# Layer 0's weight products as seven block products, and a plan with other lags, slots and tie-breaks, in a four-layer graph network

## The chip, the core and the metric

The kernel runs on one core of one Trainium2 chip. The metric is the device time of one execution in microseconds (us). The engines named below are PE (TensorE, which streams a moving operand past weights that PEld loads), DVE (VectorE), ACT (ScalarE), POOL (GpSimd) and SP, whose queue issues nearly all DMAs. The matmul outputs lie in eight PSUM banks of 128 x 512 float32.

## The reference

Input `x` is 64 graphs of 256 nodes with 128 features, float32; `adj` is one 256 x 256 matrix for all. Four layers follow one another, each with a residual and a layer norm:

```python
x = layernorm(x + L0(x, adj, adj, weight_1))   # sum over k of (adj^k x) W_k, k = 0..3, two chains
x = layernorm(x + L1(x, adj, weight, bias))    # adj (x W) + b
x = layernorm(x + L2(x, adj, W, b))            # normalised (adj + I) x W^T + b
x = layernorm(x + L3(x, adj, adj, ...))        # five gated steps, weights shared
# one step of L3
m_in = adj @ h; m_out = adj @ h; av = [m_in, m_out]
z = sigmoid(av @ w3.T + b3 + h @ u3.T + bu)
r = sigmoid(av @ w4.T + b4 + h @ u3.T + bu)
hv = tanh(av @ w5.T + b5 + (r * h) @ u5.T + bu5)
h = (1 - z) * h + z * hv
```

Both chains of L0 have the same `adj`, so the kernel adds their weights: four matrices w_0 to w_3 of 128 x 128 remain (w_0 with the identity, for the residual), and the sum is x w_0 + adj x w_1 + adj^2 x w_2 + adj^3 x w_3.

## The kernel before

Everything is float32. The 64 graphs are 32 groups of two (`NB`). A group's tile is 128 partitions x 512: two graphs, two node tiles of 128, 128 features. `Group.record` writes down a group's whole way through the four layers as operations on an engine with a cost, a lag until the result can be used, and the values they read and write. `Plan.order` then places all operations of all groups in one list: it goes from one free moment to the next and takes, over the engines, the operation that can start first, then the one of lowest rank (older groups first). Values of a kind share a fixed number of slots (`slots`: 8 banks, 48 SBUF tiles of 128 x 512 named "w", and others); a value holds its slot from its first user to its last. Each engine runs its own operations in the order of that list. Up to 10 groups (`ACTIVE`) are in flight, so PE has other groups' work while one group waits.

Layer 0, for a group. `propagate("q", x, a2T)` makes qT = (adj^2 x)^T in tile `mq`. Groups 0 and 2 (`near`, the first `HEAD` graphs) have x turned on PE (`ptx`); for the 30 others DVE turns 32 x 32 blocks (`tx`, L745), a DMA writes them to DRAM (`dx`, L748) and two DMAs bring them back as `xT` (L753), with the features in a permuted order, for which four DMAs (L308) make a permuted copy `w0p` of w_0 and w_1 at the start. Then, for each of two node tiles, a bank `py` takes x [w_0 w_1] + q [w_2 w_3], 256 columns wide: per graph one matmul with x as the stationary operand and one with q. ACT copies the right half into `v` (L771), PE adds adj v to the left half (`py<-v,aT`), and ACT copies the result to `s0` (L783). The sum is centred beforehand in the weights (`centre(w0s, w0m)` on DVE), so the layer norm needs ACT squares with an accumulator (L515), POOL's add of EPS and power -0.5 (L519, L520) and an ACT scaling (L531).

`propagate` itself is, for groups of two, `seven`: a 2 x 2 block product in seven 128 x 128 products instead of eight, with sums of x made on POOL (L614 to L621), sums of the matrix made once on DVE (`s_aT`, `s_a2T`, `s_anT`, `s_aTp`, L355 to L359), and sums of the results on DVE and ACT (L642 to L664). Its first product is an operation of its own, before the three that need POOL's sums. Layers 1 and 2 are one `seven` and one product with the weights each.

A step of layer 3: `seven` gives `mg`; bank `pr` takes w4 mg + u3 hT; ACT writes r into an SBUF tile (`gate_`, L722); DVE makes rh = r hT (L729); bank `ph` takes w5 mg and u5 rh; `pr` takes (w3 - w4) mg on top, and so holds z's argument; z and tanh are written in place into the banks; DVE forms the new hT; a DVE transpose and DMAs through DRAM bring it back with nodes on partitions (`packed`). The last `END` graphs end in `closing`, on PE, ACT, POOL and DVE.

The start: `a_nat` and x loads, then the weights, all on SP in the order of the plan; `aTp` (four DMAs at L317) is a row-permuted copy of adj's transpose for the later steps; `ahat`, `dinv`, `p_an` and `anT` are the normalised matrix for layer 2.

Of the kernel before, what the change touches and what calls it, by code (L numbers as in the profile page):

```python
# [8 lines left out]
F32 = mybir.dt.float32  # L9
# [4 lines left out]
P = 128  # L14
NB = 2
ACTIVE = 10
# [34 lines left out]
class Plan:  # L51
# [32 lines left out]
    def order(self):  # L84
# [14 lines left out]
        while any(ready.values()):  # L99
            best = None  # L100
            for e, waiting in ready.items():
                t0 = free.get(e, 0.0)
                pick = None
                for at, op in waiting:
                    need = {}
                    for v in placed[op]:
                        if v.slot is None:
                            need[v.kind] = need.get(v.kind, 0) + 1
                    short = False
# [7 lines left out]
                    key = (max(at, t0), op.rank, op.seq)  # L117
# [5 lines left out]
            (start, _, _), op = best  # L123
# [34 lines left out]
def kernel(  # L158
# [42 lines left out]
    SHAPES = {"bank": [P, 512], "x": [P, 512], "w": [P, 512], "th": [P, 384], "q": [P, P], "st": [P, Q * 6], "mv": [P, Q * 2],  # L201
              "ve": [P, Q], "rs": [P, Q]}
    slots = {"bank": BANKS, "x": ACTIVE + 3, "w": 48, "th": 10, "q": 10, "dram1": 8, "dram2": 16, "st": 12, "mv": 12, "ve": 24, "rs": 12}
# [18 lines left out]
    def fetch(rank, o, src, v, queue, after=()):  # L222
        e, cost = QUEUES[queue]
        return pre(rank, queue, cost, lambda: e.dma_start(o, src), [], [v], lag=3000, joint=True, after=after)

    def load(rank, name, shape, src, keep=True, queue="SP"):
        v = constant(name, shape) if keep else Val("w", shape, name)
        e, cost = QUEUES[queue]
        pre(rank, queue, cost, lambda: e.dma_start(v.ap, src), [], [v], lag=3000 if queue != "SP" else 2300)
        return v  # L230
# [4 lines left out]
    nc.vector.memset(half, -0.5)  # L235

# [45 lines left out]
    w0_raw = load(-1, "w0_raw", [P, C, K0], w0)  # L282
# [21 lines left out]
    w0p = constant("w0p", [P, 2, C])  # L304

    def permuted():
        for r in range(4):
            nc.sync.dma_start(w0p.ap.rearrange("(j r) k c -> r j k c", r=4)[r], w0s.ap[32 * r:32 * (r + 1), 0:2, :])  # L308

    pre(1.2, "SP", 1800, permuted, [w0s], [w0p])  # L310
# [32 lines left out]
    pre(0.3, "DVE", 600, rows, [ahat, dinv], [ahat])  # L343
    pre(0.3, "PE", 4 * 110, lambda: turn(p_an, ahat), [ahat], [p_an])
# [34 lines left out]
    raw = {name: load(0.6, f"raw_{name}", [P, src.shape[1]], src, False, "SP")  # L379
# [60 lines left out]
    class Group:  # L440
# [68 lines left out]
        def spread_of(self, tag, s):  # L509
# [3 lines left out]
            def squares():  # L513
                for q in range(self.q):
                    nc.scalar.activation(nat(y)[:, q, :], nat(s)[:, q, :], AF.Square, scale=C ** -0.5,  # L515
                                         accum_out=ve.ap[:, q:q + 1])

            def scales():
                nc.gpsimd.tensor_scalar(ve.ap, ve.ap, EPS, None, op0=OP.add)  # L519
                nc.gpsimd.tensor_tensor(rs.ap, ve.ap, half[:, :self.q], op=OP.pow)  # L520

            self.act(squares, [s], [y, ve], 295 * self.q)
            self.add("POOL", 1330, 100, scales, [ve], [ve, rs])
# [22 lines left out]
        def normalise(self, tag, s, mv, rs):  # L546
# [8 lines left out]
            return y  # L555

# [36 lines left out]
        def seven(self, tag, h, aTs, ins, blocks):  # L593
# [32 lines left out]
            def first():  # L626
                block(0, ins(h)[:, 0, 0], aTs.ap[:, 0, :P], True)

            def middle():
# [24 lines left out]
            started = self.pe(pe_cost(P, 1), first, [h, aTs], [ps])  # L654
            kept = self.act(lambda: nc.scalar.copy(row(u, 1), row(ps, 0)), [ps], [u], 165)
# [3 lines left out]
            self.pe(pe_cost(P, 3), middle, [ts, sums], [ps], True, (started,))  # L659
# [39 lines left out]
        def packed(self, name, src):  # L699
# [13 lines left out]
            self.add("SP", 900, 2300, run, [far], [t])  # L713
# [5 lines left out]
        def gate_(self, name, ps, func, bias, kept=True):  # L719

            t = self.val("w", name) if kept else ps
# [10 lines left out]
        def record(self):  # L732
            x_ = self.val("x", "x")
            plan.add("SP", 450, 4500 if self.start < HEAD else 2700, self.rank() - 1.5, lambda: nc.sync.dma_start(nat(x_), self.view(x)), [], [x_],
# [3 lines left out]
            if near:  # L738
                xT, w01 = self.copied("xT", self.transposes("x", x_)), w0s
            else:  # L740

                w01 = w0p
                turn, far = self.val("w", "tx"), self.val("dram", "dx")
                xT = self.val("w", "xT")
                self.dve(lambda: nc.vector.transpose(  # L745
                    turn.ap.rearrange("p (r b i t) -> p r b t i", r=4, t=T, i=32),
                    x_.ap.rearrange("p (b t r j) -> p r b t j", r=4, t=T, j=32)), [x_], [turn])
# [9 lines left out]
            v, s0 = self.val("w", "v"), self.val("w", "s0")  # L757
            py = []

            for t in range(T):  # L760
                p = self.val("bank", f"py0{t}")
                py.append(p)

                def first(p=p, t=t):
                    for b in range(self.nb):
                        o = p.ap[:, b * 2 * C:(b + 1) * 2 * C]
                        mm(o, (tiles if near else pairs)(xT)[:, b, t], w01.ap[:, 0:2, :], b == 0, True, shared=True)
                        mm(o, tiles(qT)[:, b, t], w0s.ap[:, 2:4, :], False, True, shared=True)

                def moved(p=p, t=t):  # L770
                    nc.scalar.copy(parts(v)[:, t], four(p)[:, :, 1, :])  # L771

                self.pe(pe_cost(2 * C, 2 * self.nb), first, [xT, qT, w01, w0s], [p])
                self.act(moved, [p], [v], 55 + 107 * self.nb)
            for t in range(T):

                def second(p=py[t], t=t):
                    for kt in range(T):
                        mm(four(p)[:, :, 0, :], aT.ap[:, kt, t * P:(t + 1) * P], parts(v)[:, kt],
                           False, True, shared=True)  # L780

                def summed(p=py[t], t=t):
# [130 lines left out]
```

## Time and profile before

| | |
|---|---|
| median of 3 runs | 1353.37 us (1351.7 to 1353.72) |
| profiled execution | 1352.22 us, of which the span from first to last instruction is 1350.3 us |
| granted PE clock | 0.999 of full |
| DVE busy | 940.9 us, 2304 instructions |
| ACT busy | 758.1 us, 2421 instructions |
| POOL busy | 680.7 us, 1097 instructions |
| DMA | 134.96 MB, 34% of 16 engines' time |
| PE busy in 0 to 10, 20 to 40, 40 to 1340, 1340 to 1350.3 us | 7.5, 17.4, 1298.2, 3.4 us |

A line of a group of instructions has the source line, the engine, output and inputs, the shape and the count; after the bar the summed busy time, the mean time of one in ns, and the engine's idle time just before them with what ended most of it. A float32 matmul stands in the trace as two passes, so an x640 in the page is 320 products; the ends of passes are modelled and overlap the next pass, so the cost of a product on PE is read from start to start. Everything before 40 us is the filling of the pipeline; after that PE's busy share is 99% to 100% in every stretch until 1340 us.

### The profile page before, as it was taken

What the parts mean: (1) busy time and instruction counts of PE and PEld (TensorE: products, weight loads), DVE (VectorE), ACT (ScalarE), POOL (GpSimd) and SP (SyncE); (2) the same over time, 40 slices, a digit from 0 to 9 for tenths busy, and PEclk for the clock granted to TensorE, in tenths of its full rate; (3) what the DMA queues carried; (4) which work ended last, traced back from release to release, by engine and by line L of the source; (5) the groups of instructions that cost most, each with busy time, mean ns of one, the idle gap of its engine ahead of it and who ended that gap; (6) DMA issues with size and microseconds to landing.
All of it is one profiled execution on the core that took longest, in us unless ns stands there. A gap on an engine that the chain in (4) does not pass through costs nothing.

```text
span 1350.3 us, 22012 instructions
## 1 busy us (share of the span) xinstructions
PE 1336.5 (99%) x6553; PEld 928.3 (69%) x6553; DVE 940.9 (70%) x2304; ACT 758.1 (56%) x2421; POOL 680.7 (50%) x1097
## 2 busy tenths in 40 slices
PE   8999999999999999999999999999999999999997
PEld 7886666676776766677666666676776776565554
DVE  5466677767667667865676776676666677877776
ACT  4675536467654556556565554474655686444445
POOL 5785425266742566247266443383653686233323
PEclk9999999999999999999999999999999999999999
DMA  6322334242522333333233433341332223333323
GB/s 175 109 71 71 94 94 128 77 128 78 147 78 77 111 95 118 115 106 100 64 110 110 127 100 98 94 137 56 110 102 63 82 85 121 87 106 95 93 78 110
DMA packets 269495, 134.96 MB, mean 100 GB/s; under 512 B 175776, under 2 KB 241056, under 8 KB 269376
## 3 DMA queue, kind: packets, MB, share of 16 engines
q1 hardware_dynamic: 269120, 133.42, 34.1%
q8 instruction: 53, 0.87, 0.3%
q14 instruction: 66, 0.54, 0.1%
q0 software_dynamic: 256, 0.13, 0.1%
HBM read 67.31 MB, written 65.80 MB: 99 GB/s over the span
## 4 chain that ended last, share of the span: by engine, by line
PE 95%; DVE 1%; DMA 1%; ACT 1%; issue 0%; SPq 0%; POOLq 0%; ACTq 0%; POOL 0%; DVEq 0%
PE pr L199 31%; PE ph L199 20%; PE pmg L199 19%; PE py L199 15%; PE pm L199 7%; PE pmq L199 3%; DMA x<-in_x_dram 1%; DMA w_raw<-in_L_gnn_weight_dram 0%; PE s L199 0%; DMA dx<-tx 0%; ACT y L515 0%; ACT y L551 0%; DVE s L543 0%; SPq L748 0%; DVE tx L745 0%
## 5 line engine op out<-in xcount | busy, mean ns | idle before, releaser
L199 PE MATMUL pr<-mg,w435u5T 128*128 128x512 f32 x640 | 319.8, 593 | 0.0
L614 POOL TENSOR_TENSOR tsg<-h 128x256 f32<-128x256 f32 x128 | 97.2, 760 | 292.5 <-DMA h<-dh 197.5
L722 ACT ACTIVATE r<-pr,bsum 128x512 f32<-128x512 f32 x160 | 109.7, 685 | 151.5 <-PE pr L199 150.7
L722 ACT ACTIVATE pr<-pr,bsum 128x512 f32<-128x512 f32 x160 | 105.5, 660 | 112.4 <-PE pr L199 109.3
L729 DVE TENSOR_TENSOR rh<-r,hT 128x512 f32<-128x512 f32 x160 | 122.7, 767 | 61.6 <-ACT r L722 60.7
L199 PE MATMUL ph<-rh,w435u5T 128*128 128x512 f32 x320 | 163.6, 594 | 0.0
L199 PE MATMUL ph<-mg,w435u5T 128*128 128x512 f32 x320 | 163.3, 592 | 0.0
L199 PE MATMUL pr<-hT,w2u3T 128*128 128x512 f32 x320 | 163.0, 593 | 0.0
L729 DVE TENSOR_TENSOR d<-ph,hT 128x512 f32<-128x512 f32 x160 | 109.7, 686 | 76.1 <-ACT ph L722 73.0
L199 PEld LDWEIGHTS pr<-mg,w435u5T 128*128 128x128 f32 x640 | 109.4, 191 | 65.3 <-issue 53.3
L722 ACT ACTIVATE ph<-ph,bsum 128x512 f32<-128x512 f32 x160 | 105.6, 660 | 60.4 <-PE ph L199 59.9
L531 ACT ACTIVATE y<-s,rs 128x128 f32<-128x128 f32 x384 | 122.1, 392 | 11.0 <-POOL rs L520 10.7
L515 ACT ACTIVATE y<-s 128x128 f32<-128x128 f32 x396 | 116.7, 299 | 16.9 <-DVE s L538 14.9
L199 PEld LDWEIGHTS pmg<-s_aTp,tsg 128*128 128x128 f32 x768 | 101.8, 192 | 33.5 <-issue 28.5
L652 DVE TENSOR_TENSOR mg<-pmg,usg 128x256 f32<-128x256 f32 x160 | 67.0, 419 | 72.7 <-PE pmg L199 70.4
L199 PEld LDWEIGHTS pmg<-aTp,h 128*128 128x128 f32 x512 | 87.1, 197 | 39.4 <-issue 29.2
L729 DVE TENSOR_TENSOR pr<-pr,d 128x512 f32<-128x512 f32 x157 | 108.7, 692 | 1.5
L520 POOL TENSOR_TENSOR rs<-ve,half 128x4 f32<-128x4 f32 x99 | 104.1, 1052 | 8.3
L519 POOL TENSOR_SCALAR ve<-ve 128x4 f32<-128x4 f32 x99 | 23.2, 234 | 166.6 <-ACT y L515 166.3
L729 DVE TENSOR_TENSOR hT<-hT,pr 128x512 f32<-128x512 f32 x157 | 106.1, 676 | 1.3
L199 PE MATMUL pmg<-s_aTp,tsg 128*128 128x128 f32 x768 | 106.2, 275 | 0.0
L642 DVE TENSOR_TENSOR usg<-usg,pmg 128x128 f32<-128x128 f32 x160 | 45.2, 284 | 81.7 <-PE pmg L199 47.7
(181 smaller groups left out, 2816.9 us busy)
## 6 DMA issues: line engine op xcount, KB each, us to landing
dh<-th SPq DMA_DIRECT2D x160, 256.0 KB, 2.0
h<-dh SPq DMA_DIRECT2D x256, 128.0 KB, 2.5
x<-in_x_dram SPq DMA_DIRECT2D x32, 256.0 KB, 3.4
hT<-dh SPq DMA_DIRECT2D x128, 64.0 KB, 2.0
out_dram<-y SPq DMA_DIRECT2D x32, 256.0 KB, 2.3
dx<-tx SPq DMA_DIRECT2D x30, 256.0 KB, 2.6
xT<-dx SPq DMA_DIRECT2D x60, 128.0 KB, 2.6
dn<-tn SPq DMA_DIRECT2D x29, 256.0 KB, 2.1
```

The costliest lines, as they stand in the source:

```text
L199: nc.tensor.matmul(o, lhsT, rhs, start=start, stop=stop, skip_group_check=shared)
L515: nc.scalar.activation(nat(y)[:, q, :], nat(s)[:, q, :], AF.Square, scale=C ** -0.5, accum_out=ve.ap[:, q:q + 1])
L519: nc.gpsimd.tensor_scalar(ve.ap, ve.ap, EPS, None, op0=OP.add)
L520: nc.gpsimd.tensor_tensor(rs.ap, ve.ap, half[:, :self.q], op=OP.pow)
L531: nc.scalar.mul(nat(y)[:, q, :], nat(s)[:, q, :], rs.ap[:, q:q + 1])
L614: nc.gpsimd.tensor_tensor(ts.ap[:, :2 * P].rearrange("p (x c) -> p x c", x=2), ins(h)[:, 1], ins(h)[:, :, 0], op=OP.subtract)
L642: nc.vector.tensor_tensor(row(u, 0), row(u, 1), row(ps, 3), op=OP.add)
L652: nc.vector.tensor_tensor(o(m, slice(1, 3)), o(ps, slice(1, 3), False), both, op=OP.add)
L722: self.act(lambda: nc.scalar.activation(t.ap, ps.ap, func, bias=bias[1], scale=1.0), [ps, bias[0]], [t], act_cost(self.width) + 100)
L729: self.dve(lambda: nc.vector.tensor_tensor(out(t), way(a), way(b), op=op), [a, b], [t])
```

## The change

- Layer 0's weight products for the 30 later groups go into a new `inner_seven`: a seven-product scheme over the 2 x 2 block of weights. DVE makes four sums of x and q (`sd`, `ss`, `se`, `sf`, in a new kind of slot "h" of 128 x 256), PE runs seven products of 128 columns per graph, and DVE and ACT put the results together in five additions and two copies. Sums of the weights (`w0t`) are made once on DVE. Groups 0 and 2 keep the old code, now in a function `inner`.
- DVE's transpose of x (now L852 of the changed kernel) reads with another order of the features, so that `xT` comes back in natural order; `w0p` and its four DMAs are gone.
- EPS goes into the squares as a bias `root` (the rows are centred, so the cross term sums to zero); POOL's addition is gone.
- In `seven` the first product joins the three behind POOL's sums.
- r of a step goes into a bank of its own instead of an SBUF tile.
- The plan: among operations of one engine that can start at the same time, one that opens no new bank comes ahead of one that does, and only then does rank count. 12 groups in flight; 38 "w" slots, 21 "h", 12 "th" and "q" in place of 48, none, 10 and 10. Costs and lags of loads, transposes and squares are other numbers. `rows` and `p_an` get later ranks.

```diff
-ACTIVE = 10
+ACTIVE = 12
...
+                        elif v.kind == "bank":
+                            opens = 0
...
-                    key = (max(at, t0), op.rank, op.seq)
+                    key = (max(at, t0), opens, op.rank, op.seq)
...
-    slots = {"bank": BANKS, "x": ACTIVE + 3, "w": 48, "th": 10, "q": 10, "dram1": 8, "dram2": 16, "st": 12, "mv": 12, "ve": 24, "rs": 12}
+    slots = {"bank": BANKS, "x": ACTIVE + 3, "w": 38, "th": 12, "q": 12, "h": 21, "dram1": 8, "dram2": 16, "st": 12, "mv": 12, "ve": 24, "rs": 12}
...
-    w0_raw = load(-1, "w0_raw", [P, C, K0], w0)
+    w0_raw = load(-1, "w0_raw", [P, C, K0], w0, lag=7300)
...
-    pre(1.2, "SP", 1800, permuted, [w0s], [w0p])
+    def w0_blocks():
+        w_0, w_1, w_2, w_3 = (w0s.ap[:, k, :] for k in range(4))
+        t1, t2, t3, t4 = (w0t.ap[:, k, :] for k in range(4))
+        nc.vector.tensor_sub(t1, w_1, w_0)
+        nc.vector.tensor_sub(t2, w_3, t1)
+        nc.vector.tensor_sub(t3, w_3, w_1)
+        nc.vector.tensor_sub(t4, w_2, t2)
+
+    pre(1.2, "DVE", 1000, w0_blocks, [w0s], [w0t])
...
-    pre(0.3, "DVE", 600, rows, [ahat, dinv], [ahat])
-    pre(0.3, "PE", 4 * 110, lambda: turn(p_an, ahat), [ahat], [p_an])
+    pre(0.9, "DVE", 600, rows, [ahat, dinv, w0s], [ahat])
+    pre(1.1, "PE", 4 * 110, lambda: turn(p_an, ahat), [ahat], [p_an])
...
                     nc.scalar.activation(nat(y)[:, q, :], nat(s)[:, q, :], AF.Square, scale=C ** -0.5,
-                                         accum_out=ve.ap[:, q:q + 1])
+                                         bias=root[:, 0:1], accum_out=ve.ap[:, q:q + 1])
...
-                nc.gpsimd.tensor_scalar(ve.ap, ve.ap, EPS, None, op0=OP.add)
...
+            self.add("DVE", 450, 400, s3, [xT], [sd])
+            self.add("DVE", 450, 400, s1, [xT, qT], [ss])
+            self.add("DVE", 450, 400, s2, [xT, ss], [st_])
+            self.add("DVE", 450, 400, s4, [qT, st_], [sf])
+
+            def opening():
+                times(half(out_, 0), at(xT, 0), w0s.ap[:, 0, :], True)
+                times(half(more, 0), whole(st_), w0t.ap[:, 1, :], True)
+                times(half(more, 1), whole(ss), w0t.ap[:, 0, :])
...
+            self.pe(pe_cost(P, 3 * NB), opening, [xT, ss, st_, w0s, w0t], [out_, more])
+            self.act(lambda: nc.scalar.copy(u1.ap, out_.ap[:, :N]), [out_], [u1], 270)
+            self.pe(pe_cost(P, NB), lambda: times(half(out_, 0), at(qT, 0), w0s.ap[:, 2, :]), [qT, w0s], [out_])
+            self.pe(pe_cost(P, NB), lambda: times(half(out_, 1), at(qT, 1), w0t.ap[:, 3, :]), [qT, w0t], [out_])
+            add(lambda: (u2.ap, u1.ap, more.ap[:, :N]), [u1, more], [u2])
+            self.pe(pe_cost(P, NB), lambda: times(half(more, 0), whole(sd), w0t.ap[:, 2, :]), [sd, w0t], [more])
+            add(lambda: (u3.ap, u1.ap, more.ap[:, :N]), [u1, more], [u3])
+            add(lambda: (half(v, 1), whole(u3), half(more, 1)), [u3, more], [v])
+            self.pe(pe_cost(P, NB), lambda: times(half(more, 1), whole(sf), w0s.ap[:, 3, :]), [sf, w0s], [more])
+            add(lambda: (half(v, 0), whole(u2), half(more, 1)), [u2, more], [v], True)
+            for t in range(T):
+
+                def second(t=t):
+                    for kt in range(T):
+                        mm(half(out_, t), aT.ap[:, kt, t * P:(t + 1) * P], half(v, kt), False, True, shared=True)
+
+                self.pe(pe_cost(N, T), second, [v, aT], [out_])
+            self.act(lambda: nc.scalar.copy(s0_t(0), half(out_, 0)), [out_], [s0], 270)
+            add(lambda: (s0_t(1), whole(u3), half(out_, 1)), [u3, out_], [s0], True)
...
-            def first():
+            def opening():
                 block(0, ins(h)[:, 0, 0], aTs.ap[:, 0, :P], True)
-
-            def middle():
                 block(2, row(ts, 0), sums.ap[:, 0, :])
...
-            t = self.val("w", name) if kept else ps
+            t = self.val("w" if kept is True else "bank", name) if kept else ps
...
-            plan.add("SP", 450, 4500 if self.start < HEAD else 2700, self.rank() - 1.5, lambda: nc.sync.dma_start(nat(x_), self.view(x)), [], [x_],
+            plan.add("SP", 450, (6000, 9000)[self.start // NB] if self.start < HEAD else 2700, self.rank() - 1.5, lambda: nc.sync.dma_start(nat(x_), self.view(x)), [], [x_],
...
-                    x_.ap.rearrange("p (b t r j) -> p r b t j", r=4, t=T, j=32)), [x_], [turn])
+                    x_.ap.rearrange("p (b t j r) -> p r b t j", r=4, t=T, j=32)), [x_], [turn], 1000)
...
+            s0 = (self.inner if near else self.inner_seven)(xT, qT)
...
-                r = self.gate_(f"r{s}", pr, AF.Sigmoid, rb)
+                r = self.gate_(f"r{s}", pr, AF.Sigmoid, rb, "bank")
```

In the changed program's order of instructions DVE makes `s_aT`, `s_a2T`, then the sums `w0s`, then `s_aTp`, and only then centres `w0s`; before, the sums and the centring of `w0s` came ahead of all four. PE takes `p_an` after the first weight products of groups 0 and 2; before, it stood ahead of them. SP's order up to the four `aTp` DMAs and the next two loads of x is unchanged.

## The prediction

> **What bounds the kernel now.** I read the page's busy times, then its chain of waits, then the list of PE's waits, then a stretch of PE's timeline from start to start, and last the first 25 us. The first two say which engine sets the time:
>
> ```profile
> PE 1336.5 (99%) x6553; PEld 928.3 (69%) x6553; DVE 940.9 (70%) x2304; ACT 758.1 (56%) x2421; POOL 680.7 (50%) x1097
> ...
> PE 95%; DVE 1%; DMA 1%; ACT 1%; issue 0%; SPq 0%; POOLq 0%; ACTq 0%; POOL 0%; DVEq 0%
> ```
>
> PE is busy 99% and carries 95% of the chain that ends last; no other engine is over 70%. A busy PE may still be slowed, so the waits of PE count (waiter, what it waited for, us in total, times, longest):
>
> ```profile
> ...
> PE pmq L199 <- ACT mq L664: 1.3, 1, 1.3
> PE p_an L259 <- DVE ahat L334: 1.2, 1, 1.2
> PE pm L199 <- DVE m L648: 1.0, 2, 0.7
> PE py L199 <- DVE m L652: 0.6, 1, 0.6
> ...
> ```
>
> The nine entries of that list add up to 6.8 us, most of it in the first 41 us. So what is taken from PE's work comes off the time, and what is added to other engines costs only what makes PE wait. The price of PE's work is the distance from one start to the next (start, duration, what runs, passes):
>
> ```profile
> 701.10 0.39 PE L199 MATMUL pmg<-s_aTp,tqg 128*128 128x128 f32 x2
> 701.33 0.39 PE L199 MATMUL pm<-aT,y 128*128 128x128 f32 x2
> 701.55 0.60 PE L199 MATMUL py<-w0p,xT 128*128 128x256 f32 x2
> 701.99 0.59 PE L199 MATMUL py<-w0s,mq 128*128 128x256 f32 x2
> 702.42 0.59 PE L199 MATMUL py<-w0p,xT 128*128 128x256 f32 x2
> ```
>
> A product of 128 columns takes 0.22 to 0.23 us of PE, one of 256 takes 0.43. Over the whole timeline the medians are 0.223, 0.432 and (512 columns) 0.859 us; products whose stationary operand is read with a step of two elements (`pmg<-aTp,h`) take 0.235.
>
> **The weight products (30 groups).** Removed: 8 products of 256 columns a group, 8 x 0.432 = 3.456 us. Added: 14 of 128 columns. Two have x itself as stationary operand, with that step of two: 2 x 0.235; the other twelve read DVE's packed sums or q: 12 x 0.223. Together 3.146 us. The second products (`py<-v,aT`, 256 columns) stay. Saved: 0.310 us a group, 9.3 us in all. Ends: if all fourteen cost 0.235, 0.166 a group, 5.0 us; if all cost 0.223, 0.334, 10.0 us. I take 9.3, since each kind has its own row.
>
> The Trainium skill speaks against this term: its page "TensorE: Matmul & The Clock Gate", section "Back-to-back issue gap", says that in a real stream of weight load and matmul pairs a product of 128 columns is spaced at about 81 ns where its columns alone need 56, because the weight load binds too. An estimate with that ratio of 1.45 on 128 columns would make fourteen products 14 x 0.216 x 1.45 = 4.4 us, more than the eight they replace, and this term +28 us instead of a saving. The rows above don't show it for these float32 pairs: 0.223 is 3% over half of 0.432.
>
> **What the new scheme puts on DVE and ACT.** DVE, a group: four sums from SBUF to SBUF, 128 x 256. The trace has 419 ns for this size with one input in a bank (`mg`, L652), and for 512 columns 767 (both in SBUF) against 686 (one in a bank), so I take 419 x 767/686 = 468 ns (ends 419 and 767); and five additions with an input in a bank, 419 each. That is 4.0 us, 119 us for 30 groups. ACT loses four copies of 370 ns and gets two. Transposes of x with the new order: the row has 699 ns, and the new reading order isn't in the trace; between no change and twice the row I take 1.0 us, +9 us (ends 0 and +21). All this lies beside PE with 12 groups in flight: DVE goes from 941 to about 1055 us, 79% of the span. Without that cover every one of the four DVE steps between q and `v` would be paid, 2 x 0.47 + 2 x 0.42 = 1.8 us a group.
>
> **Squares, EPS and r.**
>
> ```profile
> L722 ACT ACTIVATE r<-pr,bsum 128x512 f32<-128x512 f32 x160 | 109.7, 685 | 151.5 <-PE pr L199 150.7
> L722 ACT ACTIVATE pr<-pr,bsum 128x512 f32<-128x512 f32 x160 | 105.5, 660 | 112.4 <-PE pr L199 109.3
> L729 DVE TENSOR_TENSOR rh<-r,hT 128x512 f32<-128x512 f32 x160 | 122.7, 767 | 61.6 <-ACT r L722 60.7
> L729 DVE TENSOR_TENSOR d<-ph,hT 128x512 f32<-128x512 f32 x160 | 109.7, 686 | 76.1 <-ACT ph L722 73.0
> ...
> L531 ACT ACTIVATE y<-s,rs 128x128 f32<-128x128 f32 x384 | 122.1, 392 | 11.0 <-POOL rs L520 10.7
> L515 ACT ACTIVATE y<-s 128x128 f32<-128x128 f32 x396 | 116.7, 299 | 16.9 <-DVE s L538 14.9
> ```
>
> A square with a bias read from SBUF should cost what the scaling with a scale read from SBUF costs, 392 in place of 299 ns: 396 x 0.093 = 37 us of ACT. POOL loses 99 additions of 234 ns, 23 us. r into a bank: 685 to 660 ns on ACT, and rh 767 to 686 on DVE, as the in-place row and d's row show; 4 and 13 us. ACT ends near 768 us, 57%, hidden under PE but for the last group, where nothing covers it: the four squares (0.25 us apart) become four of 0.35, +0.4 us, and the addition that started 0.31 us ahead of the power goes. Tail: +0.1 us, ends 0 and +0.4.
>
> r's bank is a resource that the old trace does not show used so. One bank is held from ACT's r to the end of DVE's rh: at the end of the run 1328.19 to 1329.60, 1.4 us; 160 x 1.4 = 226 bank-us of 8 x 1350, 2%. Following every bank tile in the timeline from first matmul to last reader gives about 6.5 of 8 banks in use on average, much of it by tiles that merely lie (a `pmq` is held 42 us), and the merged first product of `seven` and the new tie-break open banks later. Ends: -1 us (all PE waits after 60 us, 0.36 + 0.3 + 0.3, gone) and +8 us (each of 160 steps loses 50 ns, a quarter of one product). I take 0, nearer to the rows, as no PE wait of the list names a bank's release.
>
> The skill's page "ScalarE: Activation LUTs", section "Step-by-step: what each stage is for", says that ACT writes faster to a bank than to SBUF, but that this is useful only if TensorE doesn't need most of the banks, which is the case here. The rows confirm the first half (25 ns); with the second half alone the sum would lean to the +8 end.
>
> **The start.** Here the change moves a due step behind another, and I expect a loss.
>
> ```profile
> 8.43 0.39 DVE L287 TENSOR_TENSOR w0s<-w_raw,ident 128x128 f32<-128x128 f32 x1 [3.27 <-DMA w_raw<-in_L_gnn_weight_dram]
> ...
> 11.07 0.69 DVE L298 TENSOR_TENSOR w0s<-w0s,w0m 128x512 f32<-128x512 f32 x1
> ...
> 18.47 0.28 DVE L355 TENSOR_TENSOR s_aTp<-aTp 128x128 f32<-128x128 f32 x1
> ```
>
> ```profile
> 9.22 2.45 SPq L317 DMA_DIRECT2D aTp<-aT  x4
> ```
>
> Now the centred `w0s` is there at 11.8 and PE starts the weight products at 14.57. In the new order the centring stands behind `s_aTp`, and that waits for the four `aTp` DMAs, whose place on SP is the same: the last is issued at 11.1 and lands 2.1 to 3.0 us later, 13.2 to 14.1. Then five DVE operations of 1.07 us in all and the centring's three of 1.53 us: `w0s` at 15.8 to 16.7, say 16.2. Until then PE has p_a (8.2), x's transposes (2 x 0.43) and two `pmq` (2 x 1.73): done at 13.0. PE then waits 3.2 us, starts the products at 16.3 instead of 14.57, and still owes `p_an` (0.65): +2.4 us, ends +1.9 and +2.9. Behind the waiting DVE queue stand `both_w`, `rows`, `wb`, `w0t` and the first transposes of x, so `dx`, the next x loads (behind `dx` on SP) and `xT` start about when they did (20.9), not earlier, although SP is rid of 2.4 us of `w0p` DMAs.
>
> Between 29 and 41 us PE now waits 1.3 + 0.7 + 0.6 + 0.3 = 2.9 us on such chains. In the new order the first seven products need `se`, which DVE makes behind two transposes that wait for x loads (3.1 to 6.9 us to landing); by the same rows `se` is ready at about 34, when PE asks for it. I put 2.0 us in place of the 2.9: -0.9, ends -2.9 (none) and +2.5.
>
> **The sum** on the profiled execution: -9.3 - 0 + 0.1 + 2.4 - 0.9 = -7.7 us, 1352.2 to 1344.5 us (span 1342.6). The median of the runs is 1.15 us above that execution, so 1353.4 - 7.7 = 1345.7 us is forecast. All low ends together: -10.0 - 1 + 0 + 1.9 - 2.9 = -12.0, 1341.4; all high ends: -5.0 + 8 + 0.4 + 2.9 + 2.5 = +8.8, 1362.2.
>
> **Rivals.**
> 1. *Everything saved, and a clean start* (1341.4 us, the low ends). For it: 12 groups give PE more to choose from, and the lags in the plan come nearer to the 3.1 to 6.9 us of the trace. Against it: the wait for `aTp` is in the program's order.
> 2. *DVE's queue becomes the wait of the first 60 us* (1352.8 us). DVE runs strictly in order; in the old start it stood 3.18 and 1.37 us before a transpose until x came. If four such stops (2 x 4.55 = 9.1 us) come through to PE in place of the 2.9: -9.3 + 2.4 - 2.9 + 9.1 + 0.1 = -0.6. For it: DVE is 98% busy from 10 to 20 us and gets nine operations more a group; against it: PE has `pm` and `pmq` of other groups then.
> 3. *Banks run out: slower.* At the opening product of a step PE waits for a bank that r or an `s0` pair holds. From 48 ns a step (7.7/160) the saving is gone, from 65 ns it is slower than can be mistaken; at 0.1 us, less than half a product, +16 us: 1361.7 us. For it: 6.5 of 8 in use, r's 160 openings; against it: no wait for banks now, and long-held banks that can give.
> 4. *The change doesn't do what it says*: excluded, as the changed order holds 14 products of 128 columns for each of the 30 groups, and PE bounds.
>
> **How the numbers follow.** A measurement of this kernel can tell 0.2% (2.7 us) from no change. Forecast (1342.5 to 1350.6): 0.66. Rival 1: 0.12, faster too. Rival 2: 0.12, within 0.2%. Rival 3: 0.10, slower. So faster 0.78, same 0.12, slower 0.10. The range 1341 to 1353.5 leaves out rival 3, a fourth of rival 2 and a fifth of rival 1: under 0.2.
>
> **What would show it.** Right: no `w0p`, products of `py` at 0.223 us from start to start, PE's busy time down 8 to 11 us; first products of group 0 at about 16.3 us, with a wait on `w0s`; r at 660 and rh near 686 ns; squares near 392 ns; DVE near 1055 us. Wrong: 128-column products in those runs above 0.24 us, a start at 14 us or earlier, PE waits of over 10 us in all after 60 us, above all waits of an opening product on DVE's rh or ACT's copies, which are bank releases.

## The result and the profile after

The changed kernel takes 1345.66 us (median of 4 runs, 1345.33 to 1345.71), the one before beside it 1353.55 us (1351.7 to 1354.08); the ratio is 0.9944, with a 95% interval of 0.9926 to 0.9961. The profiled execution took 1345.33 us with a span of 1343.5 us, against 1352.22 and 1350.3 us.

The page of the changed kernel, busy times and chain:

```profile
PE 1326.7 (99%) x6913; PEld 931.0 (69%) x6913; DVE 1046.2 (78%) x2579; ACT 773.2 (58%) x2361; POOL 638.2 (48%) x998
...
PEclk8999999999999999999999999999999999999999
...
PE 95%; DVE 2%; ACT 1%; DMA 1%; issue 0%; SPq 0%; POOLq 0%; POOL 0%; DVEq 0%; ACTq 0%
```

PE still bounds. Its busy time is 9.8 us lower, DVE's is 105 us higher and does not show in the chain. The first digit of the granted clock is new: 8, where it was 9.

PE's waits in the changed kernel:

```profile
PE py L201 <- DVE w0s L303: 4.9, 1, 4.9
PE warm L252 <- POOL ident masks.py:199: 1.4, 1, 1.4
PE pmq L201 <- DVE mq L757: 1.2, 1, 1.2
PE pm L201 <- ACT us L767: 0.7, 2, 0.6
...
```

One wait of 4.9 us at the start has come in. After 50 us the whole list is four waits of 1.5 us in all.

A group's new products in the timeline of the changed kernel (start, duration, what runs, passes; two passes are one product):

```profile
721.37 0.63 PE L201 MATMUL py<-w0s,xT 128*128 128x128 f32 x4
721.84 0.61 PE L201 MATMUL pz<-w0t,se 128*128 128x128 f32 x4
722.28 0.61 PE L201 MATMUL pz<-w0t,ss 128*128 128x128 f32 x4
722.73 1.02 PE L201 MATMUL pr<-mg,w435u5T 128*128 128x512 f32 x2
```

Two products with x take 0.47 us, two with a packed sum 0.44 or 0.45: 0.235 and 0.22 each, as the prediction took them.

To compare kernels I add up, over all products, the median distance from one start to the next for products of that size (0.223, 0.432, 0.859 us in both kernels), and call what PE needs above that sum its excess: waits, and products that run slowly. Each product of 128 columns counts 0.223 us in it, one with x as well as one with a sum. The 37 transposes at the start count as whole products, though each is a single pass; that puts the sum some 3.6 us too high and the excess of the first 50 us as much too low, in every kernel alike. The sum falls from 1327.7 to 1317.6 us. The excess grows from 4.4 to 8.9 us in PE's first 50 us, and falls from 10.0 to 8.5 us after them.

### The profile page after: what moved, and what is told of

Same layout as the page of the kernel before. It is cut to its first block, busy times and chain, and to the rows that moved or that the text cites. A ratio compares the mean times of both kernels' runs of the same rounds, so it can differ in the third digit from the quotient of the medians.

```text
span 1343.5 us, 22696 instructions
## 1 busy us (share of the span) xinstructions
PE 1326.7 (99%) x6913; PEld 931.0 (69%) x6913; DVE 1046.2 (78%) x2579; ACT 773.2 (58%) x2361; POOL 638.2 (48%) x998
## 4 chain that ended last, share of the span: by engine, by line
PE 95%; DVE 2%; ACT 1%; DMA 1%; issue 0%; SPq 0%; POOLq 0%; POOL 0%; DVEq 0%; ACTq 0%
PE pr L201 30%; PE ph L201 20%; PE pmg L201 19%; PE py L201 11%; PE pm L201 7%; PE pz L201 4%; PE pmq L201 3%; DMA x<-in_x_dram 1%; PE s L201 1%; ACT y L524 0%; DVE s L546 0%; DVE tx L852 0%; DVE ss L619 0%; ACT y L539 0%; DMA aTp<-aT 0%
## 5 line engine op out<-in xcount | busy, mean ns | idle before, releaser
L528 POOL TENSOR_TENSOR rs<-ve,half 128x4 f32<-128x4 f32 x99 | 101.3, 1023 | 205.4 <-ACT y L524 169.0
L831 ACT ACTIVATE r<-pr,bsum 128x512 f32<-128x512 f32 x160 | 105.4, 659 | 127.2 <-PE pr L201 124.9
L524 ACT ACTIVATE y<-s,root 128x128 f32<-128x128 f32 x396 | 153.7, 393 | 17.3 <-DVE s L546 15.7
L201 PEld LDWEIGHTS pmg<-aTp,h 128*128 128x128 f32 x512 | 91.9, 196 | 74.4 <-issue 47.6
L201 PEld LDWEIGHTS pr<-mg,w435u5T 128*128 128x128 f32 x640 | 105.7, 191 | 51.3 <-issue 40.3
L838 DVE TENSOR_TENSOR rh<-r,hT 128x512 f32<-128x512 f32 x160 | 108.8, 681 | 33.9 <-ACT r L831 30.5
L872 POOL TENSOR_TENSOR yb<-y,wb 128x512 f32<-128x512 f32 x64 | 83.0, 1297 | 43.5 <-ACT y L539 40.4
L201 PE MATMUL pmg<-aTp,h 128*128 128x128 f32 x512 | 98.4, 279 | 0.0
L201 PEld LDWEIGHTS ph<-rh,w435u5T 128*128 128x128 f32 x320 | 58.0, 190 | 57.1 <-issue 42.7
L201 PEld LDWEIGHTS pmg<-s_aTp,tsg 128*128 128x128 f32 x768 | 95.8, 192 | 0.0
```

Source lines behind the costliest of these rows:

```text
L201: nc.tensor.matmul(o, lhsT, rhs, start=start, stop=stop, skip_group_check=shared)
L831: self.act(lambda: nc.scalar.activation(t.ap, ps.ap, func, bias=bias[1], scale=1.0), [ps, bias[0]], [t], act_cost(self.width) + 100)
L838: self.dve(lambda: nc.vector.tensor_tensor(out(t), way(a), way(b), op=op), [a, b], [t])
L872: nc.gpsimd.tensor_tensor(nat(yb), nat(y), bias[1][:, None, :].to_broadcast([P, self.q, C]), op=OP.add)
```

## The experiments

### The start

**1. The centring of `w0s` ahead of `s_aTp`, in the changed kernel.** `late` is the operation of the five sums, `centred` that of the centring; every other place in the order stays.

```diff
+        order = plan.order()
+        order.remove(late)
+        order.insert(order.index(centred) + 1, late)
```

> The changed kernel with one operation moved in DVE's order: the five sums s_aTp stand behind the centring of w0s, nothing else moves. Theory (the 4.9 us wait of PE on w0s comes from centring behind the aTp DMAs, and it also costs the half clock of the first six products): w0s is ready near 12.3 us, the first weight products start at 12.6 to 13 us with 0.43 us from start to start and a granted clock of 1.0; 3 to 7.5 us less than the changed kernel, 1338 to 1342.5 us, the later waits for x's transposes taking back some of it. Rival (the start is set by loads of x and DVE's work, so the wait only moves to the next step): PE waits as much between 13 and 40 us, and the time is 1344 to 1346 us.

1344.41 us, ratio 0.9936 (0.9921 to 0.995). The products start at 12.81 us and at full clock, and the wait is elsewhere. PE's timeline and the windows of this kernel (stretch, PE's and PEld's, DVE's, ACT's and POOL's busy time, granted clock, DMA share, GB/s):

```profile
12.81 0.67 PE L201 MATMUL py<-w0s,xT 128*128 128x256 f32 x2
13.32 0.59 PE L201 MATMUL py<-w0s,mq 128*128 128x256 f32 x2
...
33.23 0.77 PE L201 MATMUL pmq<-s_a2T,x 128*128 128x128 f32 x2 [5.62 <-DVE mq L757]
```

```profile
30.00:40.00 10.00, 6.30 (x37) 6.14 (x38) 8.25 (x23) 4.16 (x19) 5.77 (x10) 0.66 0.85 232
```

PE idles 5.6 us for `mq`, and then runs at two thirds of its clock on average. The rival is right: what is won is 1.3 us by the medians, less than the two intervals can tell apart, and not 3 to 7.5 us. PE's excess in the first 50 us falls by 0.9 us.

**2. PE kept busy in the gap.** Forty transposes of the identity behind group 2's `pmq` fill the time until `w0s` is there; nothing reads them.

```diff
+    fill = plan.add("PE", 0, 260, -20, lambda: warming(40), [], [warm], (groups[1].square,))
...
+        order.remove(fill)
+        order.insert(order.index(groups[1].square) + 1, fill)
```

> The changed kernel with 40 transposes of the identity on PE in the 4.9 us gap before the first weight products, into a bank nobody reads; the wait on w0s stays. Theory (the idle gap lowers the granted clock, and six products at 0.86 instead of 0.43 us follow from it): clock 1.0 throughout, products start at about 17.4 us at 0.43 us each, 2.0 to 2.6 us less, 1343 to 1343.7 us. Rival (the half clock comes from elsewhere, or the slow products are hidden by later waits): no change, 1345.3 to 1346 us.

1345.48 us, ratio 0.9943 (0.9928 to 0.9957). PE's timeline:

```profile
18.52 0.67 PE L201 MATMUL py<-w0s,xT 128*128 128x256 f32 x2 [0.61 <-DVE w0s L303]
19.02 0.59 PE L201 MATMUL py<-w0s,mq 128*128 128x256 f32 x2
...
35.69 0.46 PE L201 MATMUL pmq<-s_a2T,x 128*128 128x128 f32 x2 [2.46 <-DVE mq L757]
```

The first products run 0.43 us apart instead of 0.85, so the idle time had cost the clock; but they start 1.0 us later than in the changed kernel, PE then waits 2.5 us for `mq` at 35.69 us, and nothing is won.

**3. The kernel before with the centring behind `s_aTp`.**

```diff
+        order.remove(late)
+        order.insert(order.index(centred), late)
```

> The kernel before with its centring of w0s moved behind the sums s_aTp, as the changed kernel has it; nothing else. Theory: PE waits for w0s from about 13.1 to 17 us and may lose the clock as well; 2.4 to 6.5 us slower than before, 1356 to 1360 us. Rival (order at the start is of no account since later waits absorb it): within 1 us of before.

1356.06 us, ratio 1.0023 (1.0012 to 1.0033): 3.1 us slower by the ratio, 2.3 by the medians. The products start at 17.66 us instead of 14.57, after a wait of 2.69 us, at full clock.

**4 and 5. The rows of ahat, `p_an` and anT's sums early; then two more x loads early too.**

```diff
-    pre(0.9, "DVE", 600, rows, [ahat, dinv, w0s], [ahat])
-    pre(1.1, "PE", 4 * 110, lambda: turn(p_an, ahat), [ahat], [p_an])
+    pre(0.3, "DVE", 600, rows, [ahat, dinv], [ahat])
+    pre(0.3, "PE", 4 * 110, lambda: turn(p_an, ahat), [ahat], [p_an])
...
-    def block_sums(rank, name, aTs):
+    def block_sums(rank, name, aTs, behind=()):
...
-        pre(rank, "DVE", 1200, run, [aTs], [v])
+        pre(rank, "DVE", 1200, run, [aTs, *behind], [v])
...
-    block_sums(0.7, "aTp", aTp)
+    block_sums(0.7, "aTp", aTp, [w0s])
...
-            group.load_gate = (groups[i - 2].first,)
+            group.load_gate = (groups[max(0, i - 4)].first,)
```

The last pair of lines belongs to the second of the two kernels only.

> The changed kernel with s_aTp's sums behind the centring of w0s, and with the rows of ahat, p_an, anT and the five sums of anT ahead of the centring, where DVE otherwise waits. Theory (DVE's chain up to the first mq and se sets the end of the start, and the 5 us of anT's operations between 29 and 35 us are what it is behind with): PE starts the weight products at 13 to 15 us, the wait for mq near 33 us falls from 5.6 us (with the sums behind alone) to under 2, and the time is 1341 to 1343. Rival (what sets the chain is not DVE's work but the x loads and the way through memory for xT, which stand on the same places of the queue as before): the wait moves to another row, PE waits some 5 us in all before 45 us, and the time is within 1 us of 1344.4.

> The same kernel, and besides it two more groups' x are loaded before the first way through memory instead of behind it on SP's queue. Theory (DVE's work sets the chain): no better than the kernel without the early loads, since three more transposes of 1.1 us then stand ahead of usq on DVE; 1341 to 1344. Rival (the x loads set the chain): 2 us or more faster than the kernel without the early loads, about 1340, with no stop of DVE for x between 20 and 32 us.

The first takes 1346.82 us, ratio 0.9939 (0.9927 to 0.9952), the second 1345.01 us, 0.9925 (0.9912 to 0.9937), both beside 1355.18 us of the kernel before. In PE's timeline of the first, the one wait has become two:

```profile
14.71 0.67 PE L201 MATMUL py<-w0s,xT 128*128 128x256 f32 x2 [0.86 <-DVE w0s L303]
...
30.35 0.63 PE L201 MATMUL pmq<-s_a2T,tsq 128*128 128x128 f32 x2 [1.94 <-POOL tsq L729]
33.01 0.77 PE L201 MATMUL pmq<-s_a2T,x 128*128 128x128 f32 x2 [2.03 <-DVE mq L757]
```

In the second PE waits 4.2 us for the same `mq`, behind seven transposes of x. The excess of the first 50 us is 8.1 and 7.8 us, hardly under the 8.9 of the changed kernel: for the first kernel the rival holds, by the ratio and by the waits, 4.8 us in these three rows. The second kernel is 1.8 us faster than the first by the medians, and all its times lie under all of the first's; but the profiles put the difference after the first 50 us (excess 11.0 against 8.6), so it doesn't say what the loads are worth at the start. The second kernel has the lowest ratio of all that were run. It was not timed beside the changed kernel; beside its near twin (experiment 11, in the same set of runs) it is 2.6 us faster, and the two sets of times don't overlap.

### Where the gain comes from

**6. The changed kernel with the old eight products of 256 columns.** All groups go through `inner`, with x's pairs as they now lie.

```diff
-                        mm(o, tiles(xT)[:, b, t], w0s.ap[:, 0:2, :], b == 0, True, shared=True)
+                        mm(o, (tiles if self.start < HEAD else pairs)(xT)[:, b, t], w0s.ap[:, 0:2, :], b == 0, True, shared=True)
...
-            s0 = (self.inner if near else self.inner_seven)(xT, qT)
+            s0 = self.inner(xT, qT)
```

> The changed kernel with layer 0's weights in the old form for all groups (eight products of 256 columns, x in natural order); the plan, r's bank, 12 in flight and the squares stay as changed. Theory (the seven products are the whole gain, 0.33 us a group): 9 to 11 us more than the changed kernel, 1355 to 1357 us, so slower than before by 1.5 to 3. Rival (the plan with 12 in flight and freer banks earns the time): 1346 to 1350 us.

1357.87 us, ratio 1.0038 (1.0023 to 1.0052), 12.2 us above the changed kernel: 10.0 from the spacings, and 2 from the excess (19.5 against 17.4 us). By the ratios it lies 0.0038 x 1353.6 = 5 us above the kernel before. Of its excess, 7.4 us lie in one place, between 1100 and 1150 us, where the kernel before has 0.7; so the 5 us hang on one jam in this order. So far it seems that the products are the whole gain and the rest costs 5 us. The next kernel denies that.

**7. The seven products alone, in the kernel before.** Its plan, ten groups, its squares, r in SBUF.

```diff
+            s0 = (self.inner if near else self.inner_seven)(xT, qT)
...
-    slots = {"bank": BANKS, "x": ACTIVE + 3, "w": 48, "th": 10, "q": 10, "dram1": 8, "dram2": 16, "st": 12, "mv": 12, "ve": 24, "rs": 12}
+    slots = {"bank": BANKS, "x": ACTIVE + 3, "w": 48, "th": 10, "q": 10, "h": 21, "dram1": 8, "dram2": 16, "st": 12, "mv": 12, "ve": 24, "rs": 12}
```

> The kernel before with the seven products of 128 columns alone (its own plan, ten groups in flight, its squares, its r, its centring early). Theory (the products are the whole gain, and the start in the new order costs some 4 us of it): PE's work by its spacings is 10 us under the kernel before, the weight products of group 0 start before 15 us, and the time is 1342 to 1345, at or below the changed kernel's 1345.7. Rival (the other parts, the wider window and the lags and the tie-break, are what keeps PE fed while DVE has nine operations more a group): PE's excess over the medians of its spacings grows by 3 us or more after the first 60 us, and the time is 1347 to 1353.

1360.67 us, ratio 1.0044 (1.003 to 1.0058): slower than with no change at all. The sum of the spacings is 1317.6 us, 10.0 less, as in the changed kernel; but after the first 50 us the excess is 24.5 us instead of 10.0. The theory falls, and the price is beyond what the rival gave. The start is late too: group 0's weight products begin at 16.19 us, not before 15, since PE waits 2.84 us for `ahat`. The chain of this kernel, and its PE waits from 50 us on:

```profile
PE 89%; DVE 5%; ACT 2%; DMA 2%; issue 1%; POOL 1%; SPq 0%; POOLq 0%; DVEq 0%; ACTq 0%
```

```profile
PE pmg L199 <- ACT usg L762: 1.9, 4, 0.7
PE ph L199 <- DVE rh L836: 1.6, 1, 1.6
PE pmq L199 <- ACT usq L762: 1.3, 3, 0.6
PE pr L199 <- DVE mg L759: 0.9, 2, 0.5
...
```

Ten rows of small waits, 8.4 us in all, on the chains of the propagations and of the steps. The rest of the excess are gaps and slow products that the list doesn't hold. Some other part of the change keeps PE fed. Four kernels look for it.

**8. Seven products and 12 groups in flight in the kernel before.**

```diff
-ACTIVE = 10
+ACTIVE = 12
...
-    slots = {"bank": BANKS, "x": ACTIVE + 3, "w": 48, "th": 10, "q": 10, "h": 21, "dram1": 8, "dram2": 16, "st": 12, "mv": 12, "ve": 24, "rs": 12}
+    slots = {"bank": BANKS, "x": ACTIVE + 3, "w": 38, "th": 12, "q": 12, "h": 21, "dram1": 8, "dram2": 16, "st": 12, "mv": 12, "ve": 24, "rs": 12}
```

> The seven products in the old kernel, with 12 groups in flight (and the slots that this leaves room for), without the tie-break, the new lags, the merged opening products, the squares with EPS and r's bank. Theory (the window is what the seven products need): PE's excess after 50 us falls from 25 to under 12 us and the time from 1360.7 to 1345 to 1349. Rival (another part of the plan is needed, or all of them): still 1353 or more.

1362.36 us, ratio 1.0051 (1.0038 to 1.0064). The wider window, here with ten "w" slots fewer, doesn't help: the excess after 50 us is 25.9 us.

**9. The changed kernel with 10 in flight** (`ACTIVE = 10`, all else kept).

> The changed kernel with 10 groups in flight instead of 12, all else kept. The seven products alone in the old order left PE 33 us over the medians of its spacings (17 in the changed kernel), 25 us of it after the first 50 us, in waits of 0.3 to 1.6 us on ACT's usg, DVE's m, mg and rh. Theory (the wider window is what covers the longer chains): PE's excess after 50 us rises from 8.5 to 15 us or more, and the time is 1350 or more. Rival (the window isn't what counts; the lags or the tie-break are): within 2 us of the changed kernel, a ratio near 0.994.

1348.56 us beside 1355.16, ratio 0.995 (0.9937 to 0.9962); the excess after 50 us is 10.4 us. The rival: the window isn't it. In the same set of runs the kernel with the old lags (experiment 10), which differs little from the changed one, is 2.2 us faster, and the two sets of times don't overlap: some 2 us may be the window's.

**10. The changed kernel without the preference for taken banks, and with the old lags.** Two kernels, each with one edit:

```diff
-                    key = (max(at, t0), opens, op.rank, op.seq)
+                    key = (max(at, t0), op.rank, op.seq)
```

```diff
-        return pre(rank, queue, cost, lambda: e.dma_start(o, src), [], [v], lag=8000, joint=True, after=after)
+        return pre(rank, queue, cost, lambda: e.dma_start(o, src), [], [v], lag=3000, joint=True, after=after)
...
-    raw = {name: load(0.6, f"raw_{name}", [P, src.shape[1]], src, False, lag=9000)
+    raw = {name: load(0.6, f"raw_{name}", [P, src.shape[1]], src, False)
...
-                    x_.ap.rearrange("p (b t j r) -> p r b t j", r=4, t=T, j=32)), [x_], [turn], 1000)
+                    x_.ap.rearrange("p (b t j r) -> p r b t j", r=4, t=T, j=32)), [x_], [turn])
```

> The changed kernel with the plan's key without the preference for taken banks. Theory (12 in flight covers all): within 1 us of the changed kernel, a ratio near 0.994, banks in use on average back from 4.5 towards 6.6 of 8. Rival (what feeds PE is that a group's open products are finished before new ones are begun, so that its chain starts earlier): PE's excess after 50 us rises from 8.5 to 15 us or more, and the time is 1350 or more.

> The changed kernel with the plan's former costs and lags for the loads, the ways through memory and the transposes of x. Theory (the lags bear on the start alone): within 2 us of the changed kernel, the difference within the first 60 us. Rival (the plan's truer times keep transfers ahead of PE in the whole run): PE waits more after 60 us too, and the time is 1350 or more.

With the old lags 1346.37 us, ratio 0.9933 (0.992 to 0.9947), no difference. Without the preference 1356.55 us, ratio 1.0013 (1.0005 to 1.0022; 11 runs, 1356.11 to 1358.2): slower than the kernel before, and nothing of the saving is left. By the ratios the preference is worth 0.0069 x 1353.6 = 9.3 us, by the two spans 11.3 us, and beside the kernel with the old lags, in the same set of runs, 10.2 us. The page of the kernel without it, and its PE waits from 50 us on:

```profile
PE 1332.5 (98%) x6913; PEld 933.0 (69%) x6913; DVE 1040.5 (77%) x2579; ACT 771.5 (57%) x2361; POOL 631.9 (47%) x998
...
PE 92%; DVE 4%; DMA 2%; ACT 1%; issue 1%; POOL 0%; SPq 0%; POOLq 0%; DVEq 0%; ACTq 0%
```

```profile
PE pm L201 <- ACT us L767: 1.1, 1, 1.1
PE pz L201 <- DVE v L645: 0.7, 2, 0.3
PE pr L201 <- ACT r L831: 0.6, 2, 0.3
PE ph L201 <- DVE rh L838: 0.5, 2, 0.3
PE pr L201 <- DVE mg L761: 0.5, 1, 0.5
...
```

The same 6913 instructions on PE, and PE's part of the chain falls from 95% to 92%, taken by DVE and DMA. The waits after 50 us grow from 1.5 to 4.5 us, the excess from 8.5 to 18.5. No wait names a bank. How the kernels use the banks shows when each bank tile is followed from its first matmul (r's from ACT's write) to the end of its last reader, between 50 and 1300 us:

| kernel | median, us | banks in use, mean of 8 | all 8 in use | excess after 50 us |
|---|---|---|---|---|
| before | 1353.55 | 6.6 | 22% of the time | 10.0 |
| seven products alone | 1360.67 | 6.8 | 28% | 24.5 |
| the same, 12 in flight | 1362.36 | 6.8 | 26% | 25.9 |
| changed, no preference | 1356.55 | 6.6 | 22% | 18.5 |
| changed, eight products | 1357.87 | 4.5 | under 1% | 12.7 |
| changed, 10 in flight | 1348.56 | 4.7 | 1% | 10.4 |
| changed, old lags | 1346.37 | 4.7 | under 1% | 8.7 |
| changed | 1345.66 | 4.7 | under 1% | 8.5 |

In the eight kernels that have the seven products and the preference (those of experiments 1, 2, 4, 5 and 11 too) the excess after 50 us is 8.2 to 11.0 us; in the three with the seven products and without it, 18.5 to 25.9 us. With the eight products few banks in use go with no smaller excess (12.7 us against 10.0 before).

The preference roughly halves the time that `pmq` is held (24.6 to 9.5 us), and `pz` (19.9 to 9.7) and `py` (11.9 to 6.7) likewise. Most of that is time in which a bank waits for PE's own next product: summed over all banks it falls from 3459 to 1542 us, the time before DVE's next operation from 1677 to 1277 and before ACT's from 356 to 214.

The edit reaches further than the description of the change says. `opens` is 0 only for an operation that touches a bank already taken, so an operation that works in SBUF alone is put behind as well: on DVE and ACT, among operations that can start at the same time, those on taken banks come ahead of all others. The experiment takes away both effects at once.

**11. r in SBUF again.**

```diff
-                r = self.gate_(f"r{s}", pr, AF.Sigmoid, rb, "bank")
+                r = self.gate_(f"r{s}", pr, AF.Sigmoid, rb)
```

> The changed kernel with r back in SBUF instead of a bank of its own. Theory (r's bank costs TensorE nothing and saves only covered work): the time stays within 1 us of the changed kernel's 1345.7; r goes back from 659 to about 685 ns on ACT, rh from 681 to about 767 ns on DVE, DVE's busy time rises by about 13 us, and the banks in use fall by 160 bank-us of 10,700, nothing that PE sees. Rival (r's bank is scarce and delays opening products): the kernel gets faster by 2 us or more (at 50 ns a step, 8 us). Rival of the other sign (the faster rh shortens a chain that PE waits for): slower by 2 us or more.

1347.56 us beside 1355.18, ratio 0.9944 (0.9932 to 0.9957), the ratio of the changed kernel. r is back at 685 ns, rh only at 752. r's bank is worth nothing that can be measured here (the interval of the ratio is some 1.7 us to either side). The 160 tiles of r had been held for 259 us in all, not 160: 1.5 us each in the median.

## Why the prediction was right, point by point

The forecast was 1345.7 us and the median is 1345.66, but the terms that make the sum are not those that were put down. From the span of 1350.3 us, -10.0 (spacings) + 4.5 (start) - 1.5 (excess after 50 us) + 0.2 (tail) leads to 1343.5, where -9.3 + 1.5 + 0 + 0.1 was forecast. That the medians agree within 0.04 us is luck: the profiled execution is 0.8 us above its own forecast, and it lies 0.33 us below the median, not 1.15.

**The weight products: right.** The products with x are 0.235 us apart and the others 0.22, as put down, and that is -9.3 us. The sum of the spacings shows -10.0 because it counts 0.223 for all; the other 0.7 us are in the excess. The warning that 128-column products could be bound by weight loads didn't come true.

**"Beside PE with 12 groups in flight": wrong, and this is the step that failed.** DVE's and ACT's new work was costed at nothing with the wider window named as its cover. Experiments 8, 9 and 10 show that the window is not the cover: with it, but without the preference, the seven products lose to the kernel before, and without it, but with the preference, they win, with some 2 us less at most. In the old order the seven products bring 24.5 - 10.0 = 14.5 us of excess, more than they save; the four DVE steps between q and `v` that the prediction priced at 1.8 us a group are not covered by what it named. In the new plan the preference takes 10.0 us of excess away (18.5 to 8.5); which other part takes the first 6.0 (24.5 to 18.5) was not separated.

**The bank term: 0 with ends -1 and +8 was taken for r's bank, the merged first product and the tie-break together.** For r's bank 0 is right (experiment 11). For the tie-break alone the value is -9 to -11 us, outside the ends. The hint stood in the prediction's own figure, 6.5 of 8 banks in use, "much of it by tiles that merely lie": I took it as a reserve and, as no wait named a bank, the banks as no limit. In a planned order no wait need name them, for the plan doesn't place an operation as long as it finds no free bank. Rival 3 looked for waits of opening products, and the term counted banks that open later as a cost of up to 8 us; the tie-break that opens them later is what wins. The missed loss (14.5 us) and the missed gain (16.0) nearly cancel, and so the sum came out by luck.

**The start: the wait right, the size not, and the clock left out.** +2.4 - 0.9 was put down; PE's excess in its first 50 us grew by 4.5. PE's and DVE's timeline of the changed kernel:

```profile
17.49 1.19 PE L201 MATMUL py<-w0s,xT 128*128 128x256 f32 x2 [4.94 <-DVE w0s L303]
18.47 1.06 PE L201 MATMUL py<-w0s,mq 128*128 128x256 f32 x2
19.32 1.06 PE L201 MATMUL py<-w0s,xT 128*128 128x256 f32 x2
...
22.68 0.59 PE L201 MATMUL py<-w0s,xT 128*128 128x256 f32 x2
23.11 0.59 PE L201 MATMUL py<-w0s,mq 128*128 128x256 f32 x2
```

```profile
14.26 0.29 DVE L364 TENSOR_TENSOR s_aTp<-aTp 128x128 f32<-128x128 f32 x1 [3.53 <-DMA aTp<-aT]
...
15.33 0.68 DVE L301 TENSOR_REDUCE w0m<-w0s 128x4 f32<-128x512 f32 x1
16.04 0.17 DVE L302 TENSOR_SCALAR w0m<-w0m 128x4 f32<-128x4 f32 x1
16.25 1.09 DVE L303 TENSOR_TENSOR w0s<-w0s,w0m 128x512 f32<-128x512 f32 x1
```

DVE waits for `aTp` as foreseen, until 14.26 us (13.2 to 14.1 was estimated); the last subtraction takes 1.09 instead of 0.69 us, and the wait is 4.9 instead of 3.2. Half a us of the difference is in the prediction's own sum: its terms for PE (8.2 + 0.86 + 3.46) end at 12.5 us, not 13.0, and PE was free at 12.55. Unforeseen is what follows: six products 0.85 us apart instead of 0.43, some 2.6 us, until 22.68. Windows of the changed kernel:

```profile
10.00:20.00 10.00, 5.06 (x20) 3.97 (x19) 6.37 (x17) 1.66 (x3) 3.67 (x6) 0.79 0.34 92
20.00:30.00 10.00, 10.00 (x47) 8.66 (x47) 5.99 (x13) 3.66 (x14) 1.54 (x2) 0.87 0.51 145
```

The granted clock was 0.79 and 0.87 there, against 1.00 in both stretches before. Experiment 2 removes the slow products and experiment 1 the wait, and each wins 1.3 us at most, since `mq` at 33 to 36 us is next. What sets `mq` was not settled: with the sums early the x loads, POOL's `tsq` and DVE's transposes take turns, and the excess of the first 50 us lay between 7.8 and 10.4 us in all variants of the changed kernel that have the seven products.

**The rest.** The tail took +0.2 us (+0.1 predicted). After the first 50 us PE has 1.5 us less excess, which was not in the sum; experiments 1 and 2, whose order is the same from there on, have the same excess in the same stretches (1.6 us from 450, 1.3 from 1100 us), so it belongs to the order and is no scatter. Groups of the changed kernel, each form apart (after the bar busy us and mean ns, then the idle time before), on ACT and on DVE:

```profile
L524 ACT ACTIVATE y<-s,root 128x128 f32<-128x128 f32 x396 | 153.7, 393 | 17.3 <-DVE s L546 15.7 <-DVE s L645 0.3 <-PE s L201 0.2
...
L831 ACT ACTIVATE r<-pr,bsum 128x512 f32<-128x512 f32 x160 | 105.4, 659 | 127.2 <-PE pr L201 124.9 <-DVE tn L790 1.0 <-DVE mg L757 0.2
```

```profile
L838 DVE TENSOR_TENSOR rh<-r,hT 128x512 f32<-128x512 f32 x160 | 108.8, 681 | 33.9 <-ACT r L831 30.5 <-issue 2.6 <-DMA h<-dh 0.2
...
L852 DVE STREAM_TRANSPOSE tx<-x 128x512 f32<-128x512 f32 x30 | 33.2, 1108 | 2.5 <-DMA x<-in_x_dram 2.5
...
L619 DVE TENSOR_TENSOR ss<-xT,mq 128x256 f32<-128x256 f32 x30 | 18.6, 633 | 0.1
...
L616 DVE TENSOR_TENSOR sd<-xT 128x256 f32<-128x256 f32 x30 | 15.8, 525 | 0.0
```

r (660 predicted), the squares (392) and rh (686) came as their neighbour rows said; the transposes (1.0 us) and the four sums (468 ns) were put too low, and DVE's busy time is 1046 us (1055) all the same.

## What to carry to other kernels

Work that is saved on the bounding engine is paid out only if the order keeps feeding it: test such an edit with the old order and the order with the old work, for the two together can win where each alone loses (here +6 and +5 us by the ratios, together -8). Where an order is planned with a limited resource, a shortage need not show as a wait for the resource; follow its occupancy (here eight banks, all taken for over a fifth of the time), and try an order that lets what holds one finish before another is begun. A cover named for hidden work is a claim to be tested like any other: take the cover away alone.

## What the hardware showed that was not expected

PE's clock falls with an idle time of a few us in the middle of a kernel: after 4.94 us six products ran at half speed, after 5.62 us (experiment 1) the granted clock of the next stretch was 0.66. The Trainium skill's page "TensorE: Matmul & The Clock Gate", section "What's actually happening", says that an idle window of some 3.4 us halves the clock and a busy one of that length frees it. These two rows agree, and by the page the prediction's own wait of 3.2 us was close to it. A shorter wait is less clear: after 2.69 us (experiment 3) the products ran at full clock, while after 2.46 us (experiment 2) the clock of the stretch from 30 to 40 us was 0.83, with products of 128 columns up to 0.43 us apart, and experiment 4 had 0.66 there with two waits of about 2 us. In experiment 6 two waits of 1.22 and 0.85 us, 2 us apart, at 1104 and 1106 us were followed by a product of 512 columns that took 1.70 us of PE instead of 0.86, and the granted clock from 1100 to 1110 us was 0.83. No length below which nothing is lost follows from these runs.

How the preference for taken banks shortens the waits, whether by wider choices for PE when banks are free or by chains that start earlier, is argued from the occupancy and was not separated, nor was its part on PE from that on DVE and ACT. It was not tried in the kernel before, with the eight products or with the seven; and the merged first product and the squares were not taken out alone.
